# Cross-attention's bias and mask carried in the last key row, its weights folded a tick earlier, and normalisation steps set a tick apart

## The chip, the cores and the metric

The kernel runs on one core of a Trainium2 chip. The metric is device microseconds of one execution. The median of three runs before the change is 2432.49 us (2430.0 to 2432.74). A separate execution was taken with the hardware profiler; it gives the page, the timelines and the waits quoted here. The engines are TensorE (PE in the profile, its weight loads PEld), VectorE (DVE), ScalarE (ACT), GpSimd (POOL) and SyncE (SP), which here only issues DMAs.

## What is computed

Four attention blocks in a row over x of 8 batches, 256 rows and 128 columns, with a context of 8 x 64 x 64. The first, second and last are small. The third is a stack of six layers, and nearly all of the time:

```python
def _ln(x, g, b, eps=1e-05):
    m = jnp.mean(x, axis=-1, keepdims=True)
    v = jnp.mean(jnp.square(x - m), axis=-1, keepdims=True)
    return (x - m) / jnp.sqrt(v + eps) * g + b
...
scores = jnp.einsum('bhqd,bhkd->bhqk', q, k) * D ** (-0.5)
scores = jnp.where(mask[:, None] == 0, jnp.float32(-1000000000.0), scores)
attn = jax.nn.softmax(scores, axis=-1)
...
def step(t, p):
    skv, sq, sow, sob, ckv, cq, cow, cob, w1, b1, w2, b2, pg, pb = p
    tn = _ln(t, norm_g, norm_b)
    t = _mha(tn, tn, skv, sq, sow, sob, tgt_mask) + t
    tn = _ln(t, norm_g, norm_b)
    t = _mha(src, tn, ckv, cq, cow, cob, src_mask) + t
    tn = _ln(t, pg, pb)
    t = t + (jax.nn.relu(tn @ w1 + b1) @ w2 + b2)
    return (t, None)
```

There are 16 heads of 64. Self-attention has 256 keys, cross-attention 64. All values are float32.

## The kernel before

The stream `t` stays on the chip for the whole kernel: 128 partitions by 16 tiles of 128 columns, two tiles a batch. Work on the batches is pipelined by a plan written by hand. `at(tick, phase, fn)` puts a piece of work into a tick, with a phase that orders it there. At the end the plan is walked in order of tick and phase, and each engine's instructions are chained in the order in which they were issued. So every engine has one fixed queue, and an instruction that waits holds all that stand behind it. SP is outside of this chain. A phase is only a place in the order, no time.

A layer has 48 ticks. With `T0` its first, self-attention of batch b (`plan_sa`) has T = T0 + 4b, and cross-attention (`plan_ca`) T = T_ca + 2b with T_ca = T0 + 32. The feed-forward (`plan_ff`) comes at T_ca + 2b + 7 and overlaps the next layer's self-attention.

Normalisation (`ahead`) is four steps, each with its place: `moments` (mean and variance on DVE, L808 and L809), `scales` (the root on POOL, L814 to L821; always in the tick of the moments, phase 8.4), `normal` (the rows, on ACT in L827, for self-attention on DVE in L832) and `trans` (two TensorE transposes, L841, and an ACT instruction, L843, that empties the tile and multiplies by the gain and adds the bias, one number for each partition).

Self-attention in a tick: two groups of scores (L898); on DVE an addition of the mask with a minimum (L912); exponentials on ACT (L917); the reciprocal on DVE (L925); the division on POOL (L927); a transpose on DVE (L937); and from tick T + 3 the values (L953), which DVE and ACT empty. The output projection is L971, and L978 adds its tile to the stream, at phase 8.2 of T + 6.

Cross-attention doesn't compute keys and queries. `plan_ca_weights` folds the query weights with the key weights to AT, and the value weights with the output weights to WVO (L1042, emptied by ACT in L1054 and L1052). For this the weights are transposed in blocks by DVE (L1016), stored to DRAM and fetched again, and regrouped by POOL (L1033). For each pair of batches `keys_both` multiplies AT by the context (L1079, two PSUM tiles) and ACT copies each tile to two batches' keys (L1085). The scores (L341) are normalised rows times these keys, 128 deep. The mask is added in PSUM: for each group 16 further bf16 matmuls of a row of ones with the mask's row (L348). Then `lower` copies the scores on ACT (L357), takes the maximum on DVE (L359) and subtracts it on POOL (L360); `exps` is L366, `divide` L370 to L372 a tick later, `turn` a DVE transpose (L380) two ticks later, and `sums` (L388) and the addition to the stream (L1104) three ticks later.

All PSUM tiles come from one ring of four tiles of two banks each: a tile's next use waits until the fourth-last use has been emptied. Small SBUF tiles come from rings of four, one for each name.

Of the kernel before, what the change touches and what calls it, by code (L numbers as in the profile page):

```python
# [8 lines left out]
F32 = mybir.dt.float32  # L9
# [7 lines left out]
P = 128  # L17
# [10 lines left out]
def tile_xattn_stack(ctx: ExitStack, tc: tile.TileContext, io, out: bass.AP):  # L28
# [5 lines left out]
    small = ctx.enter_context(tc.tile_pool(name="small", bufs=4))  # L34
# [120 lines left out]
    norm_b = column("L2_norm_b")  # L155
    pre_g = load_const("L2_pre_gT", [D, NL])
# [157 lines left out]
    def plan_weights_64(tick, qt, qT, keys, values, mask, take):  # L314
# [5 lines left out]
        def scores():  # L320
            sc = two_banks("sc").rearrange("p (q x) -> p q x", q=4)
            if mask is None:
# [15 lines left out]
            for q in range(4):  # L338
                qb = 4 * qt + q
                for a in range(4):  # L340
# [4 lines left out]
                        start=True, stop=False,  # L345
                    )
                for a in range(4):
                    nc.tensor.matmul(  # L348
                        sc[32 * a : 32 * a + 32, q, :], lhsT=ones0, rhs=mask,
                        start=False, stop=True,  # L350
                    )
# [24 lines left out]
        def turn():  # L376
            e = tl.pop("e").rearrange("p (q h) (k x) -> p (h k) q x", q=4, x=32)
            eT = big("k" if mask is None else "o", shape=(P, 8, 4, 32))
# [283 lines left out]
    def plan_l0(b, T):  # L662
# [69 lines left out]
        for qt in range(QT):  # L732
            plan_weights_64(
                T + qt, qt, lambda: st["q"], lambda: st["k"], lambda: st["VW"], None,
                lambda ps, qt=qt: add(qt, ps),
            )
# [113 lines left out]
    def plan_sa(l, b, T):  # L850
# [137 lines left out]
        ahead(b, (T - 6, 8.3), (T - 5, 2.6), (T - 5, 7.2), norm_g, norm_b, st, False)  # L988
# [16 lines left out]
    def plan_ca_weights(l, T):  # L1005
# [56 lines left out]
        at(T + 2, 3.6, folded("AT", 0, lambda c: st[1][:, :, c, :], HD ** -0.5))  # L1062
        at(T + 3, 3.6, folded("WVO", 1, lambda c: W["ca", l][2][:, c, :]))
# [3 lines left out]
    def plan_ca(l, b, T):  # L1067
# [3 lines left out]
        def keys_both():  # L1071

            res = [big("q", shape=(D, 4, 4, M)) for _ in range(2)]
            for g in range(2):
# [22 lines left out]
        ahead(b, (T - 4, 6), (T - 3, 2.95), (T - 2, 2.9), norm_g, norm_b, st)  # L1097
# [242 lines left out]
```

## Time and profile before

| what | value |
| --- | --- |
| median of three runs | 2432.49 us |
| the profiled execution | 2433.93 us |
| its span, first to last instruction | 2431.9 us |
| mean granted TensorE clock | 0.986 |
| mask matmuls, L348 | 1536, 274 ns mean |
| key copies, L1085 | 96, 599 ns mean |
| bias-and-gain evacuations, L843 for norm_g | 96, 571 ns mean |
| AT evacuations, L1054 | 12, 1010 ns mean |
| roots on POOL, L816 | 144, 709 ns mean |
| rows on ACT, L827 | 192, 492 ns mean; ACT idle 63.8 us before them |

The busy time of an engine is the time in which it has an instruction. On TensorE the instructions overlap in a pipeline, so a group's busy time is more than it adds to the chain. The chain of waits follows the work that ended last back to the start and gives each step to the engine and line that held it. In a timeline an entry merges equal instructions that follow each other, with their count at the end; a bracket names the idle time just before and the instruction that ended it.

### The profile page before, as it was taken

The page shows a single profiled execution, that of the slowest core. Times are in us where ns is not written, and L with a number is a line of the kernel's source. Part 1 is how long each engine was busy: PE and PEld are TensorE (multiplying, and loading weights), DVE is VectorE, ACT ScalarE, POOL GpSimd, SP SyncE. Part 2 cuts the span into 40 slices and gives each one's busy share as a digit, 9 for nine tenths or more (in the row PEclk, how much of TensorE's full clock was granted, in tenths as well). Part 3 has the DMA queues.
Part 4 walks back from the last instruction along what each step waited for, and adds up shares of the span by engine and source line. Part 5 has one row for each costly group of instructions (what it writes and reads, how often), then busy time and mean ns, then how long its engine had stood idle before and what let it go on. Part 6 is the DMA issues. An engine that isn't in the chain of part 4 may idle for free.

```text
span 2431.9 us, 99981 instructions
## 1 busy us (share of the span) xinstructions
PE 2349.5 (97%) x42411; PEld 1741.0 (72%) x42411; DVE 1836.6 (76%) x5988; ACT 1719.9 (71%) x4528; POOL 1450.3 (60%) x2483
## 2 busy tenths in 40 slices
PE   8999999999999999999999999999999999999997
PEld 4667777677777777777777777777777777777675
DVE  4778887667888667888667888667888667888674
ACT  4567777667777667777667778567778657778662
POOL 3754556755556755556765556765555765555774
PEclk9999999999999999999999999999999999999998
DMA  6000022001022001012000012000013000011000
GB/s 178 2 2 20 20 72 65 2 3 30 20 64 73 3 3 30 20 55 73 12 2 26 23 52 77 12 2 18 25 43 85 21 2 18 25 28 39 2 4 16
DMA packets 102833, 76.87 MB, mean 32 GB/s; under 512 B 8114, under 2 KB 96882, under 8 KB 102387
## 3 DMA queue, kind: packets, MB, share of 16 engines
q1 hardware_dynamic: 101794, 70.16, 10.4%
q8 instruction: 333, 5.46, 1.0%
q14 instruction: 114, 0.93, 0.1%
q10 hardware_dynamic: 592, 0.33, 0.1%
HBM read 62.07 MB, written 8.39 MB: 29 GB/s over the span
## 4 chain that ended last, share of the span: by engine, by line
PE 79%; DVE 7%; ACT 7%; POOL 5%; issue 2%; DMA 0%; SPq 0%; POOLq 0%; DVEq 0%; ACTq 0%
PE mm L861 14%; PE sc L898 14%; PE mm L953 13%; PE mm L971 7%; PE mm L880 7%; PE mm L388 5%; PE sc L341 4%; PE mm L1137 3%; PE mm L1120 3%; DVE m L359 2%; ACT e L357 2%; POOL e L360 2%; PE mm L303 1%; PE tp L841 1%; PE mm L1079 1%
## 5 line engine op out<-in xcount | busy, mean ns | idle before, releaser
L927 POOL TENSOR_SCALAR e<-e,rs 128x256 f32<-128x256 f32 x1536 | 703.1, 478 | 674.9 <-DVE rs L925 665.6
L917 ACT ACTIVATE e<-e,mn 128x256 f32<-128x256 f32 x1536 | 758.2, 495 | 133.7 <-DVE mn L912 129.4
L912 DVE CUSTOM_DVE_ANT_0 e<-sc,nm 128x256 f32<-128x256 f32 x1536 | 542.5, 419 | 108.8 <-PE sc L898 106.2
L937 DVE STREAM_TRANSPOSE eTc<-e 128x512 f32<-128x512 f32 x768 | 517.3, 695 | 62.9 <-POOL e L927 61.6
L898 PE MATMUL sc<-k,q 64*32 64x256 f32 x12288 | 378.3, 380 | 1.9 <-ACT q L867 0.9
L953 PE MATMUL mm<-eTc,v 32*64 32x256 f32 x12288 | 363.7, 378 | 5.7 <-ACT AT L1054 3.3
L953 PEld LDWEIGHTS mm<-eTc,v 32*64 32x64 f32 x12288 | 276.8, 131 | 89.1 <-issue 22.4
L360 POOL TENSOR_TENSOR e<-e,m 128x1024 f32<-128x1024 f32 x112 | 213.1, 1903 | 208.4 <-DVE m L359 208.4
L359 DVE TENSOR_REDUCE m<-sc 128x16 f32<-128x1024 f32 x112 | 136.8, 1221 | 263.8 <-ACT e L357 263.8
L898 PEld LDWEIGHTS sc<-k,q 64*32 64x32 f32 x12288 | 220.9, 106 | 123.3 <-issue 49.6
L917 ACT ACTIVATION_READ_ACCUMULATOR e<-e,mn 128x1 f32 x1536 | 287.2, 187 | 0.0
L341 PE MATMUL sc<-q,tT 128*32 128x256 f32 x3072 | 218.6, 384 | 2.3 <-DVE t L1104 2.3
L372 POOL TENSOR_TENSOR e<-e,r 128x1024 f32<-128x1024 f32 x112 | 213.0, 1902 | 1.2 <-DVE r L371 1.2
L388 PE MATMUL mm<-v,o 128*128 128x128 f32 x1536 | 199.3, 285 | 0.2 <-ACT v L309 0.2
L388 PEld LDWEIGHTS mm<-v,o 128*128 128x128 f32 x1536 | 185.6, 198 | 15.9 <-issue 8.1
L861 PE MATMUL mm<-tT,w_sk 128*128 128x256 f32 x768 | 189.1, 389 | 0.0
L971 PEld LDWEIGHTS mm<-w_sow,o 128*128 128x128 f32 x1536 | 175.1, 192 | 16.2 <-issue 12.3
L880 PE MATMUL mm<-w_sv,tT 128*32 128x256 f32 x3072 | 185.7, 382 | 0.0
L286 ACT COPY v<-mm 128x1024 f32<-128x1024 f32 x96 | 97.2, 1013 | 124.1 <-PE mm L880 123.5
L971 PE MATMUL mm<-w_sow,o 128*128 128x128 f32 x1536 | 183.4, 278 | 0.7 <-ACT WVO L1052 0.7
L861 PE MATMUL mm<-tT,w_sq 128*128 128x256 f32 x768 | 173.6, 379 | 0.0
L861 PEld LDWEIGHTS mm<-tT,w_sk 128*128 128x128 f32 x768 | 138.1, 190 | 44.1 <-issue 29.2
(212 smaller groups left out, 3551.0 us busy)
## 6 DMA issues: line engine op xcount, KB each, us to landing
nm<-mask_d SPq DMA_DIRECT2D x192, 128.0 KB
wd<-o SPq DMA_DIRECT2D x48, 128.0 KB
w_sk<-in_L_sa_kv_dram SPq DMA_DIRECT2D x6, 512.0 KB
w_sv<-in_L_sa_kv_dram SPq DMA_DIRECT2D x24, 128.0 KB
w_sq<-in_L_sa_q_dram SPq DMA_DIRECT2D x6, 512.0 KB
w_sow<-in_L_sa_ow_dram SPq DMA_DIRECT2D x6, 512.0 KB
w_ckv<-in_L_ca_kv_dram SPq DMA_DIRECT2D x12, 256.0 KB
w_cq<-in_L_ca_q_dram SPq DMA_DIRECT2D x6, 512.0 KB
```

The source lines that it names most:

```text
L341: nc.tensor.matmul(sc[32 * a : 32 * a + 32, q, :], lhsT=qT()[:, qb * 32 : (qb + 1) * 32], rhs=keys()[:, a].rearrange("p h k -> p (h k)"), ...
L360: nc.gpsimd.tensor_tensor(e, e, m.unsqueeze(2).to_broadcast([P, 16, M]), ALU.subtract)
L388: nc.tensor.matmul(ps[:, :D], lhsT=eT[:, s].rearrange("p q x -> p (q x)"), rhs=vw[:, r, k, g, :], start=(s == 0), stop=(s == 7),)
L861: nc.tensor.matmul(ps[:, i * S : (i + 1) * S], lhsT=w[:, c * P : (c + 1) * P], rhs=st["tT"], start=True, stop=True,)
L880: nc.tensor.matmul(ps[32 * a : 32 * a + 32, i, :], lhsT=st["tT"][:, kb * 32 : (kb + 1) * 32], rhs=sv[:, a].rearrange("p g x -> p (g x)"), ...
L898: nc.tensor.matmul(sc[32 * a : 32 * a + 32, r, j, :], lhsT=st["q"][g][rows, a, qb * 32 : (qb + 1) * 32], rhs=st["k"][g][rows, a, :], start ...
L912: nc.vector.tensor_tensor_reduce(e[:, i, :], sc4[:, i, :], st["nm"][:, 2 * jj + i % 2, :], -1.0, 3.0 * BIG, ALU.add, ALU.min, mn[:, i : i ...
L917: nc.scalar.activation(e[:, i, :], e[:, i, :], AF.Exp, scale=-1.0, bias=mn[:, i : i + 1], accum_out=rs[:, i : i + 1],)
L927: nc.gpsimd.tensor_scalar(e[:, i, :], e[:, i, :], rs[:, i : i + 1], 1.0, ALU.mult, ALU.mult)
L937: nc.vector.transpose(eT[:, r, :, 2 * jj : 2 * jj + 2, :], e[:, 2 * r : 2 * r + 2, :].rearrange("p j (k x) -> p k j x", x=32),)
L953: nc.tensor.matmul(ops[a // 2][r * HD : (r + 1) * HD, a % 2, :S], lhsT=st["v"][kb // 4][rows, kb % 4, (2 * g + r) * HD : (2 * g + r + 1) * ...
L971: nc.tensor.matmul(st["ps"][:, j * D : (j + 1) * D], lhsT=st["oT"][c // 4][:, c % 4, j * P : (j + 1) * P], rhs=sow[:, c, :], start=(c == 0 ...
```

## The change

Cross-attention's normalised rows no longer get gain and bias in L843. The instruction there now multiplies by `last_off` and adds `last_on`: the last of the 128 columns is replaced by one, the others stay as normalised. The gain is multiplied into AT instead (`scale`, POOL). The normalised columns add up to zero, so the last is minus the sum of the others: its row of AT is subtracted from all the others (`lose_last`, POOL). The freed last column of AT takes the bias times AT, summed over the columns (`sum_bias`, DVE, eight instructions that all write the one tile `zb`). The mask stands in the last of the 128 partitions of `nm2` and is added when the keys are copied from PSUM, on DVE. The 16 mask matmuls of each group of scores are gone.

The fold with all its steps starts at T_ca - 7. Moments, roots and rows have new places, shown below. The small rings have six tiles.

```diff
-    small = ctx.enter_context(tc.tile_pool(name="small", bufs=4))
+    small = ctx.enter_context(tc.tile_pool(name="small", bufs=6))
...
+    norm_rows = const.tile([P, 2, D], F32, tag="norm_rows", name="norm_rows")
+    for i, name in enumerate(("L2_norm_g", "L2_norm_b")):
+        nc.sync.dma_start(out=norm_rows[:, i, :], in_=io[name].partition_broadcast(P))
...
-    nm2 = const.tile([P, B, M], BF16, tag="nm2", name="nm2")
-    nc.vector.memset(nm2, 0.0)
-    ones0 = const.tile([P, 32], BF16, tag="ones0", name="ones0")
-    nc.vector.memset(ones0, 0.0)
-    nc.vector.memset(ones0[0:1], 1.0)
+    nm2 = const.tile([P, B, M], F32, tag="nm2", name="nm2")
+    last_on = ident[:, P - 1 : P]
+    last_off = const.tile([P, 1], F32, tag="last_off", name="last_off")
+    nc.vector.tensor_scalar(last_off, last_on, -1.0, 1.0, ALU.mult, ALU.add)
+    last_big = const.tile([P, 1], F32, tag="last_big", name="last_big")
+    nc.vector.tensor_scalar(last_big, last_on, -BIG, None, ALU.mult)
...
-                        start=True, stop=False,
-                    )
-                for a in range(4):
-                    nc.tensor.matmul(
-                        sc[32 * a : 32 * a + 32, q, :], lhsT=ones0, rhs=mask,
-                        start=False, stop=True,
+                        start=True, stop=True,
                     )
...
-        mi = mi[0:1, : B * M].rearrange("p (b m) -> p b m", b=B)
-        nc.sync.dma_start(out=mi, in_=io["mask_Bx1xS2_if1"].rearrange("b o m -> o b m"))
-        nc.vector.tensor_scalar(nm2[0:1], mi, 0.0, -BIG, ALU.is_equal, ALU.mult)
+        mi = mi[:, : B * M].rearrange("p (b m) -> p b m", b=B)
+        nc.sync.dma_start(
+            out=mi, in_=io["mask_Bx1xS2_if1"].rearrange("b o m -> (b o) m").partition_broadcast(P)
+        )
+        nc.vector.tensor_scalar(nm2, mi, 0.0, last_big, ALU.is_equal, ALU.mult)
...
-        ahead(b, (T - 6, 8.3), (T - 5, 2.6), (T - 5, 7.2), norm_g, norm_b, st, False)
+        ahead(b, (T - 7, 8.3), (T - 5, 2.6), (T - 5, 7.2), norm_g, norm_b, st, False)
...
+        def sum_bias():
+            st["add"] = sm([P, HC], "add")
+            z = sb([P, D], "zb", 1)
+            for c in range(HC):
+                nc.vector.tensor_tensor_reduce(
+                    z, st["AT"][:, c, :], norm_rows[:, 1], 1.0, 0.0, ALU.mult, ALU.add,
+                    st["add"][:, c : c + 1],
+                )
+
+        def scale():
+            nc.gpsimd.tensor_tensor(
+                st["AT"], st["AT"], norm_rows[:, 0].unsqueeze(1).to_broadcast([P, HC, D]), ALU.mult
+            )
+
+        def lose_last():
+            last = sm([P, HC], "last")
+            nc.gpsimd.tensor_copy(last, st["AT"][:, :, D - 1])
+            nc.gpsimd.tensor_tensor(
+                st["AT"], st["AT"], last.unsqueeze(2).to_broadcast([P, HC, D]), ALU.subtract
+            )
+            nc.gpsimd.tensor_copy(st["AT"][:, :, D - 1], st.pop("add"))
+
+        at(T + 2, 8.7, sum_bias)
+        at(T + 3, 2.35, scale)
+        at(T + 3, 8.05, lose_last)
...
-                    nc.scalar.copy(
+                    nc.vector.tensor_tensor(
                         res[i][:, :, 2 * g : 2 * g + 2, :].rearrange("p a r k -> p r a k"),
                         ps[:, :, :, i * M : (i + 1) * M],
+                        nm2[:, b + i].unsqueeze(1).unsqueeze(1).to_broadcast([P, 2, 4, M]),
+                        ALU.add,
                     )
...
-        ahead(b, (T - 4, 6), (T - 3, 2.95), (T - 2, 2.9), norm_g, norm_b, st)
+        ahead(b, (T - 5, 6), (T - 3, 0.5), (T - 2, 2.9), last_off, last_on, st)
...
-        first_at, *steps = steps or (3.1, (T - 3, 6), (T - 2, 3.3), (T - 1, 2.9))
+        first_at, *steps = steps or (3.1, (T - 3, 6), (T - 1, 0.5), (T - 1, 4.5))
...
-        plan_ca_weights(l, T_ca - 6)
+        plan_ca_weights(l, T_ca - 7)
```

The three places after the batch in `ahead` are those of moments, rows and transposes. In `plan_ca_weights` the steps keep their distances: with T its argument, the block transposes stand at T - 6 and T - 5, the fetches at T - 4 and T - 3, the regrouping at T + 1, the fold of AT at T + 2 and of WVO at T + 3.

More of the change, by code (lines that the diff above doesn't have):

```diff
@@ L312, in values_of, with plan_weights_64 @@
         return vw
-    def plan_weights_64(tick, qt, qT, keys, values, mask, take):
+    def plan_weights_64(tick, qt, qT, keys, values, halves, take):
         tl = {}
@@ L321, in scores @@
             sc = two_banks("sc").rearrange("p (q x) -> p q x", q=4)
-            if mask is None:
+            if halves:
                 for i in range(4):
@@ L377, in turn @@
             e = tl.pop("e").rearrange("p (q h) (k x) -> p (h k) q x", q=4, x=32)
-            eT = big("k" if mask is None else "o", shape=(P, 8, 4, 32))
+            eT = big("k" if halves else "o", shape=(P, 8, 4, 32))
             for i in range(2):
@@ L733, in plan_l0 @@
             plan_weights_64(
-                T + qt, qt, lambda: st["q"], lambda: st["k"], lambda: st["VW"], None,
+                T + qt, qt, lambda: st["q"], lambda: st["k"], lambda: st["VW"], True,
                 lambda ps, qt=qt: add(qt, ps),
@@ L1108, in plan_ca @@
                 T + qt, qt, lambda: st["tT"], lambda: keys_of[b], lambda: st["VW"],
-                nm2[:, b].unsqueeze(1).to_broadcast([P, 4, M]), lambda ps, qt=qt: add(qt, ps),
+                False, lambda ps, qt=qt: add(qt, ps),
             )
```

## The prediction

> **What bounds the kernel now.** I read the busy times, the chain of waits, the row of windows, and the timelines of TensorE (PE), VectorE (DVE) and ScalarE (ACT) for the first layer's fold and cross-attention. All stretches below are from that layer; the windows repeat the pattern in the other five. I number a layer's 48 ticks from 0: self-attention runs over 0 to 35, cross-attention's scores over 32 to 47.
>
> ```profile
> PE 2349.5 (97%) x42411; PEld 1741.0 (72%) x42411; DVE 1836.6 (76%) x5988; ACT 1719.9 (71%) x4528; POOL 1450.3 (60%) x2483
> ...
> PE 79%; DVE 7%; ACT 7%; POOL 5%; issue 2%; DMA 0%; SPq 0%; POOLq 0%; DVEq 0%; ACTq 0%
> ```
>
> TensorE sets the time in 79% of the span. The other 21% is the place to look: there TensorE looks busy but hangs on other engines.
>
> ```profile
> 360.00:380.00 20.00, 19.08 (x455) 13.33 (x453) 16.94 (x68) 15.72 (x52) 10.28 (x23) 1.00 0.31 80
> 380.00:400.00 20.00, 19.30 (x478) 15.59 (x482) 17.56 (x70) 18.28 (x59) 12.60 (x30) 1.00 0.28 79
> 420.00:440.00 20.00, 17.23 (x265) 12.61 (x258) 13.16 (x26) 11.31 (x17) 15.41 (x18) 0.97 0.01 2
> 439.00:440.00 1.00, 1.00 (x7) 1.00 (x6) 0.00 (x0) 1.00 (x2) 1.00 (x1) 0.50 0.00 0
> ```
>
> The columns are window, length, busy PE, PEld, DVE, ACT, POOL, granted clock, DMA share and rate. The fold (360 to 400) has DVE at 17 to 17.6 of 20 us and hardly any spare time on any of PE, DVE and ACT. In cross-attention POOL is the next busiest, and TensorE idles 2.77 us of 20.
>
> ```profile
> 372.61 1.96 PE L898 MATMUL sc<-k,q 64*32 64x256 f32 x64
> 375.33 1.96 PE L1042 MATMUL mm<-w_cq,o 64*64 64x128 f32 x32 [0.76 <-POOL o L1033]
> 380.38 3.68 PE L953 MATMUL mm<-eTc,v 32*64 32x256 f32 x120 [0.38 <-ACT AT L1054]
> 437.96 0.93 PE L841 MATMUL tp<-ident,xn 128*128 128x128 f32 x4 [2.71 <-ACT xn L827]
> 438.73 3.42 PE L388 MATMUL mm<-v,o 128*128 128x128 f32 x16
> ```
> ```profile
> 372.51 0.71 DVE L937 STREAM_TRANSPOSE eTc<-e 128x512 f32<-128x512 f32 x1 [0.20 <-POOL e L927]
> 373.81 0.42 DVE L912 CUSTOM_DVE_ANT_0 e<-sc,nm 128x256 f32<-128x256 f32 x1 [0.59 <-DMA nm<-mask_d]
> 387.78 0.42 DVE L912 CUSTOM_DVE_ANT_0 e<-sc,nm 128x256 f32<-128x256 f32 x1 [0.47 <-PE sc L898]
> 395.60 0.42 DVE L912 CUSTOM_DVE_ANT_0 e<-sc,nm 128x256 f32<-128x256 f32 x1 [0.71 <-PE sc L898]
> ```
>
> ```profile
> 447.45 0.11 PE sc L348 x4
> ```
>
> The timelines give start, duration and, in brackets, the idle time before an instruction; the last line is from the chain. DVE begins its softmax stage (L912) in ticks 28 to 31 at 373.81, 380.54, 387.78 and 395.60; only 0.5 to 0.7 us of each tick is spare. The 2.71 us stop at 437.96 is the normalised rows waiting for the roots, and it also halves the clock: the next 16 L388 matmuls take 3.42 us where an undisturbed group takes 1.95.
>
> **What the change removes.** Each cross-attention score group loses 16 mask matmuls (L348). In the chain four of them take 0.11 us (the timeline's 0.29 overlaps the next group), so 0.44 us a group, 96 groups: 42 us of TensorE time if it is the bound in each. Four key copies a pair of batches (L1085, 2.05 us) leave ACT.
>
> **What it moves without cost, and the cover.** Self-attention's moments go one tick earlier (0.79 us of DVE, rows L808 and L809). That tick has idle DVE stretches of 0.40, 0.32, 0.20 and 0.65 us, 1.4 in all; without them it costs 0.8 us a batch. The two turned weights (1.2 us of DVE each, L1016), eight stores and two fetches, and the 1.03 us regrouping move a tick earlier into ticks of the same kind; the built order of SP's queue changes only in that both halves of the next key weights stand ahead of one mask load. At most that load lands 1.4 us later (256 KB at the page's 178 GB/s), and its consumer is two ticks away. The regrouping's 0.76 us stop of TensorE goes. At the start two more broadcasts (128 KB, 0.7 us at that rate) stand behind the loads that are needed first; the key mask's load grows from 2 to 256 KB, 1.4 us once. I take 0.5 us, range 0 to 2. Six instead of four small buffers cost nothing, as the tiles only live longer.
>
> **The fold, where I expect the loss.** AT is now folded in tick 27, behind the value projection: TensorE 372.6 to 374.5, then the scores of tick 28. ACT empties it in 2.04 us (two L1054), to 376.6. DVE ends its tick, with the moments, at 373.9, and the new bias sums stand next in its queue, ahead of tick 28's L912. They wait for ACT: 2.7 us. There are eight, and each waits for the one before, since all write one scratch tile. No row shows a sum over 128 elements. Below: L912's spacing of 0.345 us for 256, less 0.13 for half the elements (255 ns against 388 between rows L1104 and L978), 0.21 each. Above: its whole 0.42 less 0.13 plus the 0.08 accumulator read, 0.37. I take 0.35, as these must drain: 2.8 us, range 1.7 to 3.0. So tick 28's stage starts at 379.4 and not 373.8, 5.6 us late. Behind it in the queue are this tick's transposes and the tile releases on which the next scores, and then values(1), wait; nothing hides it, because DVE has about 0.6 us a tick to catch up.
>
> POOL gets the scaling (1.9 us, the row of L360 for the same size) between the two divisions of tick 28, and a copy, a subtraction and a copy (0.25 + 1.9 + 0.25, with 0.2 of waits) behind them, 4.5 us. Its idle stretches there are now 2.75, 1.34 and 2.91 us. The transposes of tick 29 come out 0.9 us late; uncovered it would be 4.5.
>
> The keys' sum moves to DVE: L411, a sum from PSUM of the same size, takes 0.69 us, back to back about 0.63: 2.5 us a pair. In tick 30 this makes DVE's list 0.5 us too long. And the tile of the output projection is freed by L978, which stands behind these four sums; the second half of the next scores takes that very tile, since the ring has four. So tick 31 starts 7.0 us late, and values(1) in tick 33 7.2. Tick 34 repeats it: four sums ahead of L978 hold the scores of tick 35 for 1.55 us; three groups without a mask give back 1.3. Scores 35 end at 428.3 and not 421.2: 7.1 us lost. I allow 4.5 to 9.
>
> **Cross-attention, where I expect the gain.** From there the roots are ready a tick earlier and the 2.71 us stop goes, but TensorE does not get all of it. One round over ACT copy, DVE maximum, POOL subtraction and ACT exponential takes 1.05 + 1.3 + 1.95 + 0.95 = 5.25 us, now with 0.77 for the rows between exponential and copy; ticks 35 to 37 have 3.9 to 5.1 us of TensorE work. In tick 38 DVE has 1.15 + 1.24 + 0.2 + 1.2 + 0.2 + 2.5 + 0.8 = 7.3 us, and the feed-forward transpose waits for a tile which DVE frees. Scores 35 to 39 come to 24.85 us against 26.2: 1.35 gained, where mask, stop and slow clock together were 1.8 + 2.7 + 1.5. What is late next is the transposed weights, for which I expect a 2 us stop in tick 38. In ticks 39 to 43 TensorE is the bound again; with 0.44 a group, and POOL no longer doing two sets of roots in one tick (it held ACT 3.94 us at 464.66), the gain grows to 3.2. The 1.47 us stop at 483.69 for L832 stays (0.31 to 1.94 us an instruction; here it runs while POOL is at L360 and L372). Ticks 44 to 47 add 4 x 0.44. Together 5.0 us; I allow 3 to 8.
>
> **Sum.** 7.1 - 5.0 = 2.1 us a layer, six layers 12.6, plus 0.5: 13. The profiled run took 2433.9 us, its span 2431.9, 2.0 lying outside; it is 1.4 above the median. 2433.9 + 13 = 2447, less 1.4: 2445.5 against the median. The two bounds give (4.5 - 8) x 6 = -21 and (9 - 3) x 6 = +36.
>
> On the clock, the row comes first: 2.71 us of idling at 435 to 438 brought the clock to 0.50 in the second from 439 to 440. [...]
>
> **Rivals.** First, faster: DVE's detour is hidden, since TensorE can run four tiles ahead. For it: TensorE is 97% busy, DVE 76%. Against it: the windows of the fold, and the tile ring. Per layer the masks of ticks 32 to 34 (1.3) and the 5.0 remain: 6.3 x 6 = 38, so 2395. If ticks 35 to 39 gain their full 6.0 instead of 1.35 as well, another 4.65 x 6 = 28, it is 2367. Chance 0.30. It decides at a loss of 5.0 us a layer in the fold.
>
> Second, slower still: TensorE stands still for 4 us before values(1) in tick 29 and for 2.4 us in tick 31, and the half clock lengthens work on the path: 2 x 1.5 x 6 = 18, so 2463. For it: every layer's 2.71 us stop shows a clock of about 0.91 to 0.97 in its window. Against it: in tick 29 DVE is the later one anyway. Chance 0.14.
>
> Third, no change: cheap sums (1.7) and a shorter wait, so the fold loses about what cross-attention gains: 2432. Chance 0.13.
>
> My forecast, 2445, has 0.43; its own range is 2438 to 2458. The range 2394 to 2466 leaves out about 0.1 at each end. Differences under 0.2% (5 us) cannot be told from none. Slower 0.57, same 0.13, faster 0.30.
>
> **What would show it.** In the new profile: DVE idle some 2.7 us before the bias sums, released by ACT's AT, and the sums 2.8 us together; L912 of tick 28 about 5 us later behind its tick 27; TensorE waiting for DVE at the scores of ticks 31 and 35; no stop for the roots; L348 gone; cross-attention from scores 35 to the end of 47 about 5 us shorter. If the sums follow L937 without a wait, or DVE's stages 27 to 31 are as close as now, I am wrong and the time falls towards 2395.

## The result, and the profile after

The changed kernel takes 2450.28 us (median of four runs, 2445.69 to 2451.38), the kernel before 2431.24 beside it: a ratio of 1.0074, with an interval of 1.0059 to 1.0088. It is slower by 19 us. The profiled execution took 2451.11 us with a span of 2448.5; both are 17 above those of before. New code shifts the lines: what was L912 is now L915, L898 is L901, L953 is L956, L971 is L974, L937 is L940, L978 is L981, L827 and L832 are L830 and L835, L380 and L388 are L381 and L389, L1054 (ACT empties AT) is L1057 and L1052 (ACT empties WVO) is L1055. DVE's copy of the values, L284, is L290. New are L1071 (bias sums), L1077 (scaling) and L1087 (the last write to AT); the keys' sums are L1114. In the runs below the lines behind an edit shift again by a few.

First the page's busy times and the shares of its chain of waits.

```profile
PE 2328.8 (95%) x40875; PEld 1711.5 (70%) x40875; DVE 1903.1 (78%) x6179; ACT 1668.1 (68%) x4432; POOL 1477.4 (60%) x2507
...
PE 74%; DVE 11%; POOL 8%; ACT 5%; issue 2%; DMA 0%; SPq 0%; POOLq 0%; DVEq 0%; ACTq 0%
```

The 1536 mask matmuls are gone, and TensorE is less busy by 21 us. Yet its share of the chain fell from 79 to 74%, and DVE's rose from 7 to 11%: the time freed on TensorE did not come off the end, because more of the path now runs over DVE and POOL. The fold shows it in DVE's timeline (start, duration, idle time before and its releaser; the reads of the accumulator between the lines are left out).

```profile
377.03 0.29 DVE L1071 CUSTOM_DVE_ANT_0 zb<-AT,norm_rows 128x128 f32<-128x128 f32 x1 [3.08 <-ACT AT L1057]
...
377.37 0.29 DVE L1071 CUSTOM_DVE_ANT_0 zb<-AT,norm_rows 128x128 f32<-128x128 f32 x1
...
379.63 0.42 DVE L915 CUSTOM_DVE_ANT_0 e<-sc,nm 128x256 f32<-128x256 f32 x1
...
398.70 2.45 DVE L1114 TENSOR_TENSOR q<-mm,nm 128x512 f32<-128x512 f32 x4
...
402.35 0.39 DVE L981 TENSOR_TENSOR t<-mm,tb 128x256 f32<-128x256 f32 x1
402.66 0.41 DVE L915 CUSTOM_DVE_ANT_0 e<-sc,nm 128x256 f32<-128x256 f32 x1
```

DVE stands still 3.08 us for AT. The eight sums follow 0.335 us apart, so tick 28's softmax stage starts at 379.63 and not at 373.81, and that of tick 31 at 402.66 and not at 395.60. In tick 30 the four keys' sums (2.45 us) stand ahead of L981, which frees the output projection's tile. TensorE's timeline has the other half.

```profile
381.24 1.10 PE L901 MATMUL sc<-k,q 64*32 64x256 f32 x32 [2.23 <-DVE mn L915]
...
385.28 0.66 PE L956 MATMUL mm<-eTc,v 32*64 32x256 f32 x8 [1.56 <-ACT WVO L1055]
386.31 5.37 PE L956 MATMUL mm<-eTc,v 32*64 32x256 f32 x120 [0.37 <-ACT WVO L1055]
...
420.10 5.47 PE L974 MATMUL mm<-w_sow,o 128*128 128x128 f32 x32 [1.52 <-DVE o L290]
...
446.30 2.02 PE L389 MATMUL mm<-v,o 128*128 128x128 f32 x16 [1.91 <-DVE o L381]
```

TensorE waits 2.23 us at the scores of tick 29 until DVE has read a tile, then 1.56 for the evacuation of WVO, which stands in ACT's queue behind tick 28's exponentials. The 120 values behind this take 5.37 us where before they took 3.68; the output projection of tick 34 takes 5.47 instead of 3.74. The windows (length, busy times, then the clock) say why: the granted clock is 0.66 in both places, and by the microsecond it is 0.50 from 388 to 390 and from 422 to 424. The microseconds beside these have 0.58 and 0.72, and 0.65 and 0.65; the fifth has 1.00. So each five give 1.7 us less than they would at 1.00, and the two stretches of matmuls take 1.69 and 1.73 us longer than before.

```profile
386.00:391.00 5.00, 4.69 (x112) 3.76 (x116) 4.57 (x20) 4.97 (x19) 4.91 (x7) 0.66 0.02 3
420.00:425.00 5.00, 4.90 (x29) 4.90 (x30) 3.66 (x9) 2.42 (x3) 4.67 (x8) 0.66 0.05 12
```

The 2.71 us stop for the roots is gone. In tick 38 one of 1.91 us for transposed weights (L381) has come.

To compare many kernels I cut each layer at four marks on TensorE: the first self-attention score, the last one, the first cross-attention score and the last one. Means of layers 2 to 5, where all kernels have the same tick plan, in us:

| kernel | self-attention scores, with the fold | to the first cross-attention score | cross-attention scores | to the next layer | layer |
| --- | --- | --- | --- | --- | --- |
| before | 246.2 | 3.6 | 114.5 | 7.8 | 372.1 |
| after | 251.3 | 4.7 | 110.4 | 7.7 | 374.0 |

So the fold loses 5.1, the hold behind the keys' sums 1.1, cross-attention gains 4.2 and the step to the next layer 0.1: 1.9 us a layer lost. When layer 2 begins, 3.4 us are lost (0.3 of them before tick 27 of the first layer), and the last layer with the end loses 5.5, since its cross-attention gains next to nothing (112.3 before, 112.1 after). The sum, 3.4 + 4 x 1.9 + 5.5, is the 16.5 us of span.

### The profile page after: what moved, and what is told of

It reads as the page before. It is cut to its first block, busy times and chain, and to the rows that moved or that the text cites. A ratio compares the mean times of both kernels' runs of the same rounds, so it can differ in the third digit from the quotient of the medians.

```text
span 2448.5 us, 97012 instructions
## 1 busy us (share of the span) xinstructions
PE 2328.8 (95%) x40875; PEld 1711.5 (70%) x40875; DVE 1903.1 (78%) x6179; ACT 1668.1 (68%) x4432; POOL 1477.4 (60%) x2507
## 4 chain that ended last, share of the span: by engine, by line
PE 74%; DVE 11%; POOL 8%; ACT 5%; issue 2%; DMA 0%; SPq 0%; POOLq 0%; DVEq 0%; ACTq 0%
PE mm L864 14%; PE sc L901 13%; PE mm L956 12%; PE mm L883 7%; PE mm L974 7%; PE mm L389 6%; PE sc L347 3%; PE mm L1168 3%; PE mm L1151 3%; POOL e L930 2%; DVE e L915 2%; DVE m L360 2%; POOL e L361 2%; PE mm L309 2%; DVE r L371 1%
## 5 line engine op out<-in xcount | busy, mean ns | idle before, releaser
L915 DVE CUSTOM_DVE_ANT_0 e<-sc,nm 128x256 f32<-128x256 f32 x1536 | 542.6, 419 | 88.3 <-PE sc L901 87.3
L940 DVE STREAM_TRANSPOSE eTc<-e 128x512 f32<-128x512 f32 x768 | 515.7, 695 | 59.8 <-POOL e L930 58.2
L901 PE MATMUL sc<-k,q 64*32 64x256 f32 x12288 | 381.3, 382 | 19.2 <-DVE mn L915 14.7
L956 PE MATMUL mm<-eTc,v 32*64 32x256 f32 x12288 | 375.8, 384 | 18.1 <-ACT WVO L1055 9.5
L956 PEld LDWEIGHTS mm<-eTc,v 32*64 32x64 f32 x12288 | 283.1, 134 | 108.5 <-issue 25.1
L901 PEld LDWEIGHTS sc<-k,q 64*32 64x32 f32 x12288 | 221.8, 107 | 139.5 <-issue 63.1
L389 PEld LDWEIGHTS mm<-v,o 128*128 128x128 f32 x1536 | 180.4, 193 | 45.1 <-issue 39.1
L389 PE MATMUL mm<-v,o 128*128 128x128 f32 x1536 | 196.3, 281 | 15.8 <-DVE o L381 15.0
L974 PEld LDWEIGHTS mm<-w_sow,o 128*128 128x128 f32 x1536 | 181.6, 198 | 25.4 <-issue 12.3
L974 PE MATMUL mm<-w_sow,o 128*128 128x128 f32 x1536 | 190.1, 284 | 9.1 <-DVE o L290 9.1
L347 PE MATMUL sc<-q,tT 128*32 128x256 f32 x3072 | 185.7, 382 | 4.4 <-DVE t L1135 2.2
L367 ACT ACTIVATE e<-e 128x1024 f32<-128x1024 f32 x112 | 118.3, 1056 | 100.5 <-POOL e L361 100.1
## 6 DMA issues: line engine op xcount, KB each, us to landing
w_ckv<-in_L_ca_kv_dram SPq DMA_DIRECT2D x12, 256.0 KB
```

The lines of the kernel that those rows point to most:

```text
L347: nc.tensor.matmul(sc[32 * a : 32 * a + 32, q, :], lhsT=qT()[:, qb * 32 : (qb + 1) * 32], rhs=keys()[:, a].rearrange("p h k -> p (h k)"), ...
L389: nc.tensor.matmul(ps[:, :D], lhsT=eT[:, s].rearrange("p q x -> p (q x)"), rhs=vw[:, r, k, g, :], start=(s == 0), stop=(s == 7),)
L901: nc.tensor.matmul(sc[32 * a : 32 * a + 32, r, j, :], lhsT=st["q"][g][rows, a, qb * 32 : (qb + 1) * 32], rhs=st["k"][g][rows, a, :], start ...
L915: nc.vector.tensor_tensor_reduce(e[:, i, :], sc4[:, i, :], st["nm"][:, 2 * jj + i % 2, :], -1.0, 3.0 * BIG, ALU.add, ALU.min, mn[:, i : i ...
L940: nc.vector.transpose(eT[:, r, :, 2 * jj : 2 * jj + 2, :], e[:, 2 * r : 2 * r + 2, :].rearrange("p j (k x) -> p k j x", x=32),)
L956: nc.tensor.matmul(ops[a // 2][r * HD : (r + 1) * HD, a % 2, :S], lhsT=st["v"][kb // 4][rows, kb % 4, (2 * g + r) * HD : (2 * g + r + 1) * ...
```

## The experiments

Each kernel was timed in five rounds beside the kernel before. Times are medians.

**The sums and the scaling a tick later.**

```diff
-        at(T + 2, 8.7, sum_bias)
-        at(T + 3, 2.35, scale)
+        at(T + 3, 5, sum_bias)
+        at(T + 3, 7, scale)
```

> The changed kernel with one move: the eight bias sums go from the end of tick 27 to tick 28 behind the two L912 groups and the first reciprocal, and the scaling on POOL behind them. Nothing else differs. Theory (DVE waits for AT at the head of its queue): the 3.08 us of waiting goes, the 2.7 us of sums stay; tick 28's softmax stage starts about 375.9 instead of 379.6, and TensorE's stop before the scores of tick 29 shrinks with its half clock. About 3 to 4.5 us a layer, 2423 to 2432 us. Rival (the key sums on DVE are the loss, the wait is hidden): within 5 us of 2450.

2436.93 us, 1.0023 of before (1.0013 to 1.0033): 13 us better than the change, so the place of the sums is most of the loss, but not all of it; the theory had 5 us more. DVE's timeline:

```profile
377.78 0.42 DVE L915 CUSTOM_DVE_ANT_0 e<-sc,nm 128x256 f32<-128x256 f32 x1 [2.09 <-PE sc L901]
...
381.82 0.26 DVE L1071 CUSTOM_DVE_ANT_0 zb<-AT,norm_rows 128x128 f32<-128x128 f32 x1
```

The sums now follow without a wait. But DVE's stage of tick 28 waits 2.09 us, for TensorE: the scores of that tick stand behind AT's 32 matmuls (1.96 us), which the earlier tick has put between the value projection and them. With WVO behind, ACT's evacuation still stops the values for 1.25 + 0.37 us. This is a cost of the fold's place itself. The values of tick 29 are still slow in layer 2 (5.37 us), but not in layer 3 (3.68). TensorE in layers 2 and 3:

```profile
755.82 5.37 PE L956 MATMUL mm<-eTc,v 32*64 32x256 f32 x120 [0.37 <-ACT WVO L1055]
...
1130.08 3.68 PE L956 MATMUL mm<-eTc,v 32*64 32x256 f32 x120 [0.37 <-ACT WVO L1055]
```

The self-attention scores take 249.0 us in layer 2 and 249.1 in layer 3. So in tick 29 the slow values cost nothing that the layer shows. I read this so: DVE is later there anyway.

**A slice of scratch for each sum.**

```diff
-            z = sb([P, D], "zb", 1)
+            z = sb([P, HC, D], "zb", 1)
...
-                    z, st["AT"][:, c, :], norm_rows[:, 1], 1.0, 0.0, ALU.mult, ALU.add,
+                    z[:, c, :], st["AT"][:, c, :], norm_rows[:, 1], 1.0, 0.0, ALU.mult, ALU.add,
```

> The changed kernel with a slice of scratch for each of the eight sums, so that none waits for the one before. Theory (they drain one by one: 0.335 us apart where 0.22 would be the work): 0.9 us a layer less, 2443 to 2447. Rival (the spacing is the instruction's own and the accumulator read's, not the common tile's): no change, 2449 to 2452.

2444.97 us, 1.0054 (1.0037 to 1.0071). DVE's timeline:

```profile
379.18 0.29 DVE L1071 CUSTOM_DVE_ANT_0 zb<-AT,norm_rows 128x128 f32<-128x128 f32 x1 [3.08 <-ACT AT L1057]
...
379.40 0.29 DVE L1071 CUSTOM_DVE_ANT_0 zb<-AT,norm_rows 128x128 f32<-128x128 f32 x1
...
380.88 0.42 DVE L915 CUSTOM_DVE_ANT_0 e<-sc,nm 128x256 f32<-128x256 f32 x1
```

The sums are 0.21 us apart and not 0.335, 0.9 us less for the eight: that each waits for the one before through the one tile is shown by the rows. What it is worth at the end is less sure. The medians differ by 5 us as expected, but the two intervals overlap, and the profiled execution (2451.78 us) is the slowest of its six: there the self-attention scores are 0.5 us a layer shorter and cross-attention 0.8 longer.

**The fold back in its old ticks.**

```diff
-        plan_ca_weights(l, T_ca - 7)
+        plan_ca_weights(l, T_ca - 6)
```

> The changed kernel with the whole fold a tick later again, where the kernel before had it (AT in tick 28, WVO in tick 29); sums, scaling and subtraction follow AT as in the change, so in ticks 28 and 29. Theory (the tick further ahead is itself part of the loss: in tick 27 AT's matmuls stand ahead of the scores of tick 28, whose softmax stage then starts 1.9 us later even without the sums, and DVE waits 3.1 us for ACT): DVE's stage of tick 28 starts as before, the sums find AT nearly ready and cost 2.7 less the 0.6 of slack, the keys' sums 1.4 more: some 4 us lost in the fold instead of 8.9, so 2450 less 4.9 x 6 = 29: 2421 to 2432. Rival (the earlier tick was needed, since POOL has not finished AT when tick 30 multiplies it by the context): TensorE stops 3 us or more for POOL in tick 30, 2443 to 2460.

2459.74 us, 1.0114 (1.0099 to 1.013): slower than the change, and the rival holds in its time and place (its stop is 2.35 us; I had said 3 or more). TensorE's timeline:

```profile
389.10 1.93 PE L1045 MATMUL mm<-w_cow,o 64*64 64x128 f32 x30 [1.02 <-DVE mn L915]
...
399.46 0.71 PE L1108 MATMUL mm<-ctx,AT 64*128 64x128 f32 x8 [2.35 <-POOL AT L1087]
```

The keys' product of tick 30 waits 2.35 us until POOL has finished AT. With the work placed behind AT the earlier tick is needed; in its old place the fold has no room for it.

**The same work on the weights, before the fold.** AT is linear in the transposed query weights. So the bias sums, the scaling and the lost row can be done on these weights, and nothing has to follow AT.

```diff
+        def by_d(row):
+            return row.rearrange("p (i x) -> p i x", x=32)
...
+        def sum_bias(c0):
+            if c0 == 0:
+                st["add"] = sm([P, HC], "add")
             z = sb([P, D], "zb", 1)
-            for c in range(HC):
+            for c in range(c0, c0 + 2):
                 nc.vector.tensor_tensor_reduce(
-                    z, st["AT"][:, c, :], norm_rows[:, 1], 1.0, 0.0, ALU.mult, ALU.add,
-                    st["add"][:, c : c + 1],
+                    by_d(z), st[1][:, :, c, :], by_d(norm_rows[:, 1]), 1.0, 0.0, ALU.mult,
+                    ALU.add, st["add"][:, c : c + 1],
                 )
...
-                st["AT"], st["AT"], norm_rows[:, 0].unsqueeze(1).to_broadcast([P, HC, D]), ALU.mult
+                st[1], st[1],
+                by_d(norm_rows[:, 0]).unsqueeze(2).to_broadcast([P, 4, HC, 32]), ALU.mult,
...
-            nc.gpsimd.tensor_copy(last, st["AT"][:, :, D - 1])
+            nc.gpsimd.tensor_copy(last, st[1][:, 3, :, 31])
...
-        plan_ca_weights(l, T_ca - 7)
+        plan_ca_weights(l, T_ca - 6)
```

The first version put the steps two ticks ahead of the fold:

```diff
-        at(T + 1, 8.05, regrouped)
+        at(T, 8.05, regrouped)
...
+        for i in range(3):
+            at(T - 2 + i, 8.7, lambda i=i: sum_bias(2 * i))
+        at(T + 1, 2.25, lambda: sum_bias(6))
+        at(T + 1, 2.35, scale)
+        at(T + 1, 8.05, lose_last)
```

> The changed kernel with the gain and bias of the normalisation and the missing last row worked into the transposed weights from which AT is made, before the fold and not after it: the eight sums go two a tick into ticks 24 to 27, POOL scales and subtracts in tick 27, the regrouping goes to tick 26, and the fold is back in ticks 28 and 29. The same result and the same number of operations. Theory (the loss of the fold is the detour behind AT: its wait, its sums in one piece, and the place of the fold): what is left is the keys' sums, 2 to 2.5 us a layer, against the 5.9 us that cross-attention gains in the first five layers and nothing in the last: 5 x (2.3 - 5.9) + 2.3 = -16, 2416, allowed 2410 to 2424. Rival (it is the keys' sums on DVE that cost, by the tile that the output projection keeps): the fold still loses 5 us or more a layer, 2430 to 2440.

2459.05 us, 1.0115 (1.0098 to 1.0133). Both theories missed, by my own placing. TensorE's timeline:

```profile
381.62 3.68 PE L1045 MATMUL mm<-w_cq,o 64*64 64x128 f32 x32 [5.73 <-POOL w_cq L1093]
385.23 3.01 PE L901 MATMUL sc<-k,q 64*32 64x256 f32 x64
```

POOL's scaling sits between the two divisions of tick 27, its subtraction behind the second, and the fold waits 5.73 us for it; then its 32 matmuls take 3.68 us and the scores 3.01, where each took 1.96 before. I had put the sums in ticks where DVE has room, but POOL's two operations a tick too late. The second version sets them right:

```diff
-            at(T - 6 + i, 8.7, lambda i=i: turned(i))
-            at(T - 4 + i, -0.5, lambda i=i: fetched(i))
+            at(T - 7 + i, 8.7, lambda i=i: turned(i))
+            at(T - 5 + i, -0.5, lambda i=i: fetched(i))
         at(T + 1, 8.05, regrouped)
...
+        for i in range(4):
+            at(T - 4 + i, 8.03 if i == 3 else 8.7, lambda i=i: sum_bias(2 * i))
+        at(T - 1, 8.05, scale)
+        at(T, 8.05, lose_last)
```

> As the run with the weights worked early, but everything on them a tick or two earlier still: turned and fetched a tick earlier, two sums a tick in ticks 22 to 25, the scaling behind the second division of tick 25, the subtraction behind that of tick 26, the regrouping in tick 27 as in the kernel before; the fold in 28 and 29. Theory (that run's fold stood still 5.7 us for POOL's w_cq, and the half clock that followed cost 1.7 and 1.1 us on the fold and the scores behind it; without that the detour behind AT costs nothing): 2459 less 8.5 x 6 = 51: 2408, allowed 2402 to 2420. Rival (POOL's two more operations of 2 us make the divisions late wherever they stand, or the keys' sums hold the fold at its loss): 2428 to 2445.

2418.62 us, 0.9944 of before (0.9929 to 0.9958): inside what was allowed, and faster than both kernels. In its timeline of TensorE the fold looks as it did before the change:

```profile
377.62 1.96 PE L1045 MATMUL mm<-w_cq,o 64*64 64x128 f32 x32 [0.83 <-POOL o L1036]
...
382.61 3.68 PE L956 MATMUL mm<-eTc,v 32*64 32x256 f32 x120 [0.38 <-ACT AT L1057]
...
399.41 0.91 PE L956 MATMUL mm<-eTc,v 32*64 32x256 f32 x24 [0.80 <-DVE t L981]
```

The stop of 0.83 for the regrouping is the old one, the values of tick 29 take 3.68 us as before the change, and only the 0.80 behind the keys' sums is new. The sums cost DVE 0.8 to 1.0 us in each of four ticks, and the self-attention scores still take 245.9 us: there the ticks have room for it.

**The output sum ahead of the keys' sums**, with the first and the second version of the early weights.

```diff
-        at(T + 6, 8.2, add_out)
+        at(T + 6, 3.65, add_out)
```

> The kernel with the weights worked early, and besides self-attention's output sum (which frees the tile of the output projection) placed ahead of the keys' sums in ticks 30 and 34. Theory (that tile holds the next scores while four sums of 0.6 us stand ahead of its release): 1.4 us a layer less than without this, some 8 us, 2404 to 2416. Rival (DVE is simply full in those ticks, whichever sum comes first; or the output projection is not ready then and DVE waits for it): within 3 us of the run without it, or slower.

> The same with self-attention's output sum ahead of the keys' sums in ticks 30 and 34. Theory: 2446.5 (the run with both) less 5.3 + 1.8 us of stop and half clock in each layer, 43: 2403, allowed 2396 to 2412; some 8 to 12 us faster than the run without the moved output sum. Rival (what held the keys was the late fold, so that with the fold on time the order of these sums does not matter): within 3 us of the run without it.

The first gives 2446.52 us (1.0061, 1.0046 to 1.0076), 12.5 better than without, where 8 were expected, and still far from the time forecast. The second gives 2417.62 (0.9937, 0.9922 to 0.9952), no better than 2418.62: there the rival holds. The second kernel's timeline of TensorE:

```profile
400.61 1.93 PE L347 MATMUL sc<-q,tT 128*32 128x256 f32 x32
...
406.63 4.21 PE L956 MATMUL mm<-eTc,v 32*64 32x256 f32 x128 [1.86 <-DVE eTc L940]
```

Cross-attention's first score comes 3.6 us after the last self-attention score instead of 5.0, but the next values then wait 1.86 us for DVE instead of 0.92, and cross-attention takes 112.3 us instead of 110.4. The 1.4 us are handed back within two ticks.

**Three edits on the changed kernel.** Sums and scaling later, separate slices, and the output sum first.

> The changed kernel with its fold in ticks 27 and 28, and three edits: the sums and the scaling a tick later (2437 alone), a slice of scratch for each sum (5 us alone), the output sum ahead of the keys' sums (12.5 us, in the run with the weights worked early). Theory (the three act at different places, ticks 27 to 29 and 30 to 34, so they add up): 2437 less 12 less 3: 2422, allowed 2417 to 2429. Rival (with the sums out of the way TensorE is bound by the place of the fold itself: 1.9 us of it ahead of the scores of tick 28, and a stop of 1.6 us and the half clock behind WVO, so the other two are hidden): 2433 to 2438.

2429.65 us, 0.9988 (0.9976 to 1.0), 0.65 us outside what the theory allowed and 3 from the rival. The three together give 21 us, but the fold keeps 2.1 us a layer (248.3 us of self-attention scores). The slow values of tick 29 have no part in it: they take 3.68 us in layer 2 and 5.35 in layer 5, and the self-attention scores as a whole take the same there, to 0.1 us.

**The old places of the normalisation steps, in the changed kernel.**

```diff
-        ahead(b, (T - 7, 8.3), (T - 5, 2.6), (T - 5, 7.2), norm_g, norm_b, st, False)
+        ahead(b, (T - 6, 8.3), (T - 5, 2.6), (T - 5, 7.2), norm_g, norm_b, st, False)
...
-        ahead(b, (T - 5, 6), (T - 3, 0.5), (T - 2, 2.9), last_off, last_on, st)
+        ahead(b, (T - 4, 6), (T - 3, 2.95), (T - 2, 2.9), last_off, last_on, st)
...
-        first_at, *steps = steps or (3.1, (T - 3, 6), (T - 1, 0.5), (T - 1, 4.5))
+        first_at, *steps = steps or (3.1, (T - 3, 6), (T - 2, 3.3), (T - 1, 2.9))
```

> The changed kernel with moments, rows and transposes at their old places; fold, mask and small rings as changed. Theory (the moved places bring the gain in ticks 35 to 47): the 2.71 us stop for the rows is back in tick 38, with its half clock, and POOL has two sets of roots in a tick: 2 to 4 us a layer slower, 2462 to 2474 us. Rival (the rows in ACT's round and the feed-forward transpose at the end of a tick cost more than they bring): below 2445 us.

2490.08 us, 1.0238 (1.0222 to 1.0253): the direction is the theory's, but 16 us more than it allowed. The list of TensorE's waits (total, times, longest):

```profile
PE tp L844 <- ACT xn L830: 55.8, 30, 3.2
```

In the kernel before, this row has 20.6 us in 13 waits. Without the masks TensorE comes to the transposes earlier and waits longer: so I read it. The new places are worth 40 us in the changed kernel.

**The new places alone, in the kernel before**, with the six small buffers.

> The kernel before with only the moved moments, rows and transposes and the small rings of six; the mask stays in matmuls, keys on ACT, fold at its old place. Theory: the stop for the rows goes in each layer and nothing is paid in the fold: 1.5 to 3.5 us a layer, 2410 to 2422 us. Rival (the places themselves cost): 2436 us or more.

2431.76 us, 1.000 (0.999 to 1.0011): no change at all; the theory missed. TensorE's timeline:

```profile
440.18 2.02 PE L388 MATMUL mm<-v,o 128*128 128x128 f32 x16 [1.40 <-DVE o L380]
443.41 2.06 PE L1079 MATMUL mm<-ctx,AT 64*128 64x128 f32 x32 [0.18 <-ACT tT L843]
446.94 0.64 PE L341 MATMUL sc<-q,tT 128*32 128x256 f32 x8 [1.11 <-DVE t L1104]
```

The 2.71 us stop for the rows is gone, and in the same stretch stand 1.40 + 0.18 + 1.11 = 2.69 us of others. The slow matmuls behind it are gone too (these 16 take 2.02 us and not 3.42). Yet cross-attention takes 114.3 us a layer where it took 114.5. The stop only had a new name. I read this so: in these ticks the round over ACT, DVE and POOL sets the pace, and TensorE waits for it at one place or another. The last experiment bears on it.

**The keys copied on ACT, as before the change.** This kernel doesn't add cross-attention's mask.

```diff
-                    nc.vector.tensor_tensor(
+                    nc.scalar.copy(
                         res[i][:, :, 2 * g : 2 * g + 2, :].rearrange("p a r k -> p r a k"),
                         ps[:, :, :, i * M : (i + 1) * M],
-                        nm2[:, b + i].unsqueeze(1).unsqueeze(1).to_broadcast([P, 2, 4, M]),
-                        ALU.add,
                     )
```

> The changed kernel with the keys copied by ACT as before, so the cross-attention mask is not added at all; the rest is as changed. Theory (the bias sums and their wait are the larger loss): DVE's list of tick 30 is 2.5 us shorter and L978 no longer stands behind four sums, 2 to 3 us a layer, 2432 to 2438 us. Rival (the key sums are the loss): 5 us a layer or more, at most 2420 us.

2457.93 us, 1.0104 (1.0088 to 1.012): 8 us slower than with the sums on DVE, and both theories missed. ACT's timeline:

```profile
452.70 2.05 ACT L1114 COPY q<-mm 128x512 f32<-128x512 f32 x4 [0.19 <-PE mm L1108]
454.61 0.60 ACT L846 ACTIVATE tT<-tp,L_pre_bT,L_pre_gT 128x256 f32<-128x256 f32 x1
455.08 1.08 ACT L367 ACTIVATE e<-e 128x1024 f32<-128x1024 f32 x1
```

Here the copies hold the exponential of the round by 2 us: it starts at 455.08, in the changed kernel at 452.44. Cross-attention takes 112.1 us instead of 110.4. The hold ahead of the first cross-attention score seems to go (3.6 us instead of 4.7 in all layers but the fourth), but the self-attention scores take 252.7 us, 1.4 more. It has only moved, as TensorE's timeline shows:

```profile
402.00 1.10 PE L901 MATMUL sc<-k,q 64*32 64x256 f32 x32 [1.00 <-DVE t L981]
```

The second half of tick 31's scores now waits for L981. Together the two columns are 256.5 us here and 256.0 in the changed kernel.

**The round made shorter.** On the better version of the early weights, ACT makes the rows behind its copy of the scores, and cross-attention's residual goes from POOL to DVE.

```diff
-    def residual(b, bias):
+    def residual(b, bias, engine=None):
...
-        nc.gpsimd.tensor_tensor(
+        (engine or nc.gpsimd).tensor_tensor(
...
-            st["tb"] = residual(b, W["ca", l][3])
+            st["tb"] = residual(b, W["ca", l][3], nc.vector)
...
-        ahead(b, (T - 5, 6), (T - 3, 0.5), (T - 2, 2.9), last_off, last_on, st)
+        ahead(b, (T - 5, 6), (T - 3, 2.05), (T - 2, 2.9), last_off, last_on, st)
...
-        first_at, *steps = steps or (3.1, (T - 3, 6), (T - 1, 0.5), (T - 1, 4.5))
+        first_at, *steps = steps or (3.1, (T - 3, 6), (T - 1, 2.05), (T - 1, 4.5))
```

> The fastest run so far (weights worked early, 2418.6) with two edits in cross-attention: the rows are normalised on ACT behind the copy of the scores and not between exponential and copy, and cross-attention's residual plus bias (0.74 us a batch) goes from POOL to DVE. Theory (without the masks the bound of ticks 36 to 41 is the round over ACT's copy, DVE's maximum, POOL's subtraction and ACT's exponential, some 6.0 us a tick with 0.86 us of rows in it, and POOL's own list, 6.1 us in ticks with a residual; TensorE has 5.5 or less): about 0.5 us a tick in three or four ticks, 1.5 to 2 us a layer, 2409, allowed 2404 to 2414. Rival (TensorE waits for DVE's transposes there, and DVE gets 0.4 us more to do): no gain, 2416 to 2422.

2401.33 us, 0.9869 of before (0.9848 to 0.989): 17 us gained where about 10 were expected, outside the allowed range, and the fastest of all. What it started from can be seen in ACT's timeline of the run before it:

```profile
441.32 1.06 ACT L367 ACTIVATE e<-e 128x1024 f32<-128x1024 f32 x1 [3.37 <-POOL e L361]
442.28 0.86 ACT L830 ACTIVATE xn<-t,nm,rstd 128x128 f32<-128x128 f32 x2
443.05 0.99 ACT L358 COPY e<-sc 128x1024 f32<-128x1024 f32 x1
```

The rows stand between the exponential of one group and the copy of the next, and ACT had idled 3.37 us for POOL before. In the new kernel's timeline of TensorE the stops of this place are 1.17 and 0.35 us instead of 1.92 and 1.12:

```profile
440.06 2.02 PE L389 MATMUL mm<-v,o 128*128 128x128 f32 x16 [1.17 <-DVE o L381]
...
446.15 1.93 PE L347 MATMUL sc<-q,tT 128*32 128x256 f32 x32 [0.35 <-DVE t L1142]
```

Some of the gain looks like clock: layers 1 to 5 now take 106.8 us of cross-attention each, where before layers 2 and 5 took 111.15 and the others 109.6. In layer 2, at 851.90, 32 score matmuls took 3.17 us there, where most groups take 1.93. I ran the two edits together, so their shares stay open. The layers of all experiments, cut as above:

| kernel | self-attention scores, with the fold | to the first cross-attention score | cross-attention scores | layer |
| --- | --- | --- | --- | --- |
| sums and scaling later | 249.2 | 4.7 | 110.8 | 372.4 |
| a slice for each sum | 250.8 | 4.7 | 111.1 | 374.3 |
| three edits | 248.3 | 3.6 | 112.4 | 371.9 |
| fold back | 251.9 | 4.7 | 111.6 | 375.7 |
| old places | 253.5 | 5.7 | 115.6 | 382.5 |
| new places alone | 246.4 | 3.6 | 114.3 | 372.0 |
| keys on ACT | 252.7 | 3.8 | 112.1 | 376.3 |
| weights early, POOL late | 252.5 | 5.0 | 109.9 | 375.1 |
| the same, output sum first | 251.1 | 3.6 | 111.1 | 373.4 |
| weights early | 245.9 | 5.0 | 110.4 | 369.0 |
| the same, output sum first | 246.0 | 3.6 | 112.3 | 369.5 |
| weights early, shorter round | 246.7 | 5.0 | 106.8 | 366.2 |

## Why the prediction was right, and where not

The forecast was 2445 us, slower by 13; it is slower by 19, and by 16.5 in the profiled executions. Of these, layers 2 to 5 lose 1.9 each (forecast 2.1), the start and the first layer 3.4 (2.6), the last layer 5.5 (2.1). The direction and the mechanism of the fold are as forecast. Point by point:

- **The wait and the sums.** I had 2.7 us of waiting and 2.8 of sums, and tick 28's stage at 379.4. The rows show 3.08, 2.6 (eight sums 0.335 apart, less what the last need not wait) and 379.63. That each sum waits for the one before through the common tile is shown by the run with separate slices, whose 0.21 us spacing is the lower bound of the prediction.
- **Tick 31.** Its stage was forecast 7.0 us late and is 7.06 late (402.66 against 395.60). The way there is in part another. I had the second half of tick 31's scores waiting for the output projection's tile. They run without a stop, and L915 follows L981 with no idle time: DVE's own queue is what is late. The tile holds the values behind the scores instead (0.50 us, TensorE at 402.80 for L981).
- **The fold as a whole, 7.1 us at the end of the scores of tick 35.** My terms, 7.2 + 1.55 - 1.3, make 7.45. It is 8.9 in the first layer (430.4 against 421.2 before, less the 0.34 us by which this layer is late already). The 1.55 us stop at the scores of tick 35 isn't there. TensorE stops for DVE in tick 34 instead, 0.57 us for the maximum and 1.52 for DVE's copy of the values, and the output projection behind them takes 5.47 us instead of 3.74, at a granted clock of 0.66 from 420 to 425. This 1.7 us is the largest term that I had not in the sum. The mechanism is that of the second rival, which I had set as a case of its own, before other work (the values of ticks 29 and 31) and twice a layer, 18 us. It came on the path once a layer, in layers 1, 3, 5 and 6; in 2 and 4 the output projection takes 3.84 us. At 1.6 us each that makes 6 to 7 us, an estimate. In tick 29 it is covered, as I had said against this rival.
- **What the loss is made of.** I put 5.6 us on the wait and the sums alone. Moving them away gave back 13 us, 2.2 a layer. The rest of the fold's loss is the place: AT's matmuls ahead of the scores of tick 28 (DVE waits 2.09 us for them) and WVO's evacuation. I had named the first of these in a clause and not priced it, since it lay under the longer wait. Once nothing followed AT and the fold was in its old place, the self-attention scores took 245.9 us against 246.2 before: the whole 5.1 us is the detour with its place, and none of it the load that the sums put on DVE.
- **The keys' sums.** The hold through the output projection's tile is there, 1.1 to 1.4 us in the step to the first cross-attention score. But I gave nothing for taking the copies off ACT; the run with the copies there shows that the move as a whole gains 8 us.
- **Cross-attention, 5.0 us.** From tick 35 on it is 5.9 in the first layer. With 8.9 lost in the fold this leaves a loss of 3.0 from tick 27 on, so two errors, 1.8 and 0.9, partly offset: that is luck. In layers 2 to 5 the net loss of 1.9 is near what I had for every layer, 2.1. The stop of 2 us for transposed weights in tick 38 was forecast; it is 1.91.
- **"Six layers".** This step failed: in the last layer cross-attention gains 0.2 us. One reason is in the trace of the kernel before. I had said that every layer's 2.71 us stop slows the clock. In the last layer it doesn't: the 16 matmuls behind it take 1.95 us, where layers 1 to 5 show 2.9 to 3.5, and the clock is 1.00 from 2296 to 2301. So up to 1.5 us that I counted as a gain were not there to be had. In the changed kernel TensorE also stops more: from 18 to 73 us behind the layer's first cross-attention score 5.5 us in all, against 4.3 before. Its feed-forward stands at other ticks; whether that is the reason was not tried.
- **What the parts do for each other.** I took the stop for the rows and the mask matmuls as two gains to be added. The new places alone gave 0.2 us, which is nothing, and the changed kernel without them loses 40. So they pay only in the changed kernel. That the matmuls of the masks had filled the time in which TensorE would wait for the round is how I read this; no run removes the masks alone.
- **The rivals.** A hidden detour (2395) is refuted by the wait in the trace. The half clock is real (0.50 from 422 to 424), at about a third of its price (the 6 to 7 us above, of 18). No change would have needed cheaper sums: the run with slices had them and was still slower.

## What to carry over

When work has to be put behind an instruction that ends late, look for the same algebra on its operand: what is linear can be done on the weights ticks earlier, and the path stays as it was. Moving a whole step ahead also moves its matmuls ahead of others in the queue; price them, even where a longer wait covers them now. When a stop is removed from a stretch that a round over several engines bounds, it can come back under another name, as here: add up all stops of the stretch, and shorten the round instead.

## What the runs showed of the hardware

In the first layer of the changed kernel the granted clock, by the microsecond, was 0.58, 0.50, 0.50 and 0.72 from 387 to 391, and 0.65, 0.50, 0.50 and 0.65 from 421 to 425, with 1.00 around both. Ahead of this stood stops of TensorE that were short and broken: 2.23, 0.28, 1.56 and 0.37 us in tick 29, and 0.57 and 1.52 in tick 34. It did not fall each time. Behind the same two stops of tick 34 the output projection took 5.47 us in layers 1, 3, 5 and 6 and 3.84 in layers 2 and 4, where the clock stayed at 1.00. In these two it fell behind the 1.91 us of tick 38 instead (0.50 from 821 to 824 and from 1569 to 1571; 16 matmuls in 2.55 and 3.03 us, 2.02 in the first layer), and cross-attention took 109.5 and 109.6 us. Layers 1, 3 and 5 took 111.1 to 111.2, though in layer 5 it fell in tick 38 as well (0.50 from 1944 to 1947, 2.44 us). So it is the place of the fall that counted: in tick 34 it cost 1.5 us, in ticks 29 and 38 nothing that the layer shows (for tick 29, the 249.0 and 249.1 us of the kernel with the sums later).

A product with a sum over 128 elements on DVE started every 0.21 us in the kernel with a slice for each sum, and every 0.335 us in the changed kernel, where all write one tile. The instruction took 0.29 us in both, but in the kernel with the sums later it took 0.44 to 0.49 from 382.1 to 384.0, where POOL's division ran from 382.00 to 383.93, and 0.29 again at once behind it. In that stretch the sums started 0.48 to 0.54 us apart, about the length of one of POOL's four instructions (1.93 us together).
